# The first two batches' transposed activations and row of means: one by squares, one over memory, with ScalarE's work moved behind four projection steps

## The chip, the cores and the metric

The kernel runs on one core of a Trainium2 chip. Five engines work side by side and each executes its own instructions in order: TensorE (PE; its weight loads are listed as PEld), VectorE (DVE), ScalarE (ACT), GpSimd (POOL), and SyncE (SP), which here only issues DMAs. They are tied together by semaphores. The metric is the device time of one launch in microseconds, as the median of the runs shown.

## The reference

The input x has shape (16, 1024, 256), the adjacency `adj` is 1024x1024, everything is float32. Layer 0 is an attention whose queries come from a graph product; layer 1 is a two-layer graph network with batch norms. Both end in a residual and a layer norm. The change lies in the first microseconds of layer 0:

```python
fea = jnp.transpose(x, (0, 2, 1))
c_adj = jnp.mean(fea, axis=1)                       # mean of each node's 256 features
diff = c_adj[:, None, :] - c_adj[:, :, None]
A = jnp.abs(jnp.abs(jax.nn.sigmoid(diff) - 0.5) - 0.5) * 2.0
A_s = (A + jnp.transpose(A, (0, 2, 1))) * 0.5
Wg = adj[None, :, :] * A_s                          # 1024x1024 weights for each batch
g = jnp.einsum('bcn,bnm->bcm', fea, Wg)
g = jax.nn.relu(g * para.reshape(1, C, N))          # becomes the queries
kv = (x @ kv_w).reshape(B, N, 2, h, hd).transpose(2, 0, 3, 1, 4)
attn = jax.nn.softmax(jnp.einsum('bhnd,bhmd->bhnm', q, k) * scale, axis=-1)
```

The kernel computes the weights as abs(c_m - c_n), then tanh of half of it, then (tanh - 1) times the adjacency, with the sign put right later.

## The kernel before

`fast_path` does the work (`general_path` is a fallback that these inputs don't take). The 1024 nodes of a batch are 8 chunks of 128 partitions. For each batch `b` a function `prologue(b)` builds three lists of steps: `first` (the batch's x transposed, its means), `steps` (the projections: `values` and `keys`, four of each, and for batch 0 the graph product `graph_first`, eight chunks), and `side` (`weights_abs` and `weights_tanh` on ScalarE and `weights_adj` on VectorE for each of the eight chunks: the 128x1024 tiles `wg`). The main loop runs attention of batch b in bursts of two units (`scores` on PE, exp on ScalarE, `outputs` on PE, sums on VectorE) and works off the lists of batches b+1 and b+2 between the bursts. For batches 0 and 1 there is no attention to hide behind yet, so their lists are run in a block ahead of the loop, lines 1332 to 1348. There PE, ScalarE, VectorE and SP run exactly in the order of the program text, since the block stands under `manual_schedule`; GpSimd's order is left to a planner.

How the pieces concerned are made:

- **Means.** `begin` sums x over its features on VectorE (L796, `csum`), scales the sum to the column of means `ccol` (L798), and, for all batches but 0, to a negative copy in `ncol` (L801), which `column_to_row` transposes (L777) and writes to memory with four small DMAs (L780, `c`); a fifth DMA (L804) reads the row back into all 128 partitions as `crow`. For batch 0 the row is made by PE instead: `row_of_means` (L830) multiplies the transposed x by a constant matrix `ncmat`, eight matmuls into a PSUM tile.
- **Transposed x** (`xT`). For batches 0 and 1, `transpose_x` does four groups of four 128x128 PE transposes (L811), each group copied out of PSUM (L815) by VectorE, or by ScalarE for two groups of batch 1. From batch 2 on, `load_squares` (L764) loads x in 32x32 squares by four DMAs for each of two halves, and `transpose_squares` (L820) transposes a half in one VectorE instruction. Both halves pass through one buffer (tag `xS`, one deep), so the second load waits for the first transpose.
- **Buffers.** `wg` has eight buffers, so a tile of batch 1 can be begun only when PE is through with the same chunk of batch 0. Each of the PSUM tags `s`, `t`, `o` has two buffers; `values`, `keys` and `transpose_x` share tag `t`. VectorE copies batch 0's values out of PSUM (L1011), ScalarE the keys (L997).
- **Loads.** SP issues x of batch 0 in two halves, the projection weights `kvw_s`, two adjacency chunks, x of batch 1, the other six adjacency chunks and `para_s`, all ahead of the first step.

In the block before the loop, PE's order is: four transpose groups of batch 0, the row of means, four `values` and four `keys` in turn, four transpose groups of batch 1, the 64 matmuls of `graph_first` (L978), then batch 1's `values` and `keys`, then the first scores. ScalarE's and VectorE's weight steps are laid between these two at a time.

Of the kernel before, what the change touches and what calls it, by code (L numbers as in the profile page):

```python
# [10 lines left out]
F32 = mybir.dt.float32  # L11
# [7 lines left out]
P = 128  # L19
HALF = 512  # L20
# [495 lines left out]
def fast_path(  # L516
# [19 lines left out]
    nc = tc.nc  # L536
    B, N, C = x.shape
    H = 4
    D = C // H
    NCH = N // P  # L540
    CC = C // P
# [4 lines left out]
    const = ctx.enter_context(tc.tile_pool(name="const", bufs=1))  # L546
# [13 lines left out]
    def tile_s(name):  # L560
        return psum["s"].tile([P, N], F32, tag="s", name=name)

    def tile_t(name):
        return psum["t"].tile([P, HALF], F32, tag="t", name=name)
# [17 lines left out]
    make_identity(nc, ident)  # L582
    ones = const.tile([P, D], F32, name="ones")
    nc.gpsimd.memset(ones, 1.0)
    ncmat = const.tile([P, P], F32, name="ncmat")
    nc.gpsimd.memset(ncmat, -1.0 / C)
    mhalf = const.tile([P, NCH], F32, name="mhalf")
    nc.gpsimd.memset(mhalf, -0.5)

# [120 lines left out]
    def load_columns():  # L710
        for name, src, k in (
            ("b1", b1, HC), ("g1", g1, HC), ("be1", be1, HC),
            ("b2", b2, CC), ("g2", g2, CC), ("be2", be2, CC),
        ):
            cols[name] = const.tile([P, k], F32, name=f"col_{name}")
            nc.gpsimd.dma_start(cols[name], src.rearrange("(k p) -> p k", p=P))
# [9 lines left out]
    crp = graph.enter_context(tc.tile_pool(name="crp", bufs=1))  # L726
# [8 lines left out]
    with (  # L735
# [9 lines left out]
        adj_s = adjp.tile([P, NCH, N], F32, tag="adj", name="adj_s")  # L745
        para_s = pap.tile([P, CC, N], F32, tag="pa", name="para_s")
# [3 lines left out]
        def load_x(b):  # L750
            t = xp.tile([P, NCH, C], F32, tag="x", name=f"x_{b}")
            src = x[b].rearrange("(n p) c -> p n c", p=P)
            if b == 0:
                for n in range(0, NCH, 4):
                    nc.sync.dma_start(t[:, n : n + 4, :], src[:, n : n + 4, :])
            else:
                nc.sync.dma_start(t, src)
            st[b] = {"x": t}

        def load_squares(b, c):  # L760
            xs = st[b]["xS", c] = xsp.tile([P, N // SQ, SQ], F32, tag="xS", name=f"xS_{b}_{c}")
            src = x[b].rearrange("(j k) (c q i) -> c q k j i", k=SQ, q=NQ, i=SQ)
            for q in range(NQ):
                nc.sync.dma_start(xs[q * SQ : (q + 1) * SQ], src[c, q])  # L764
# [1 line left out]
        load_x(0)  # L766
        nc.sync.dma_start(kvw_s, kv_w.rearrange("(c p) k -> p c k", p=P))
        adj_src = adj.rearrange("(n p) m -> p n m", p=P)
        for n in range(0, NCH, 2):
            nc.sync.dma_start(adj_s[:, n : n + 2, :], adj_src[:, n : n + 2, :])  # L770
            if n == 0:
                load_x(1)
        nc.sync.dma_start(para_s, para.rearrange("o (c p) i j -> p (o c) (i j)", p=P))
        load_columns()

        def column_to_row(row_d):
            nc.vector.transpose(ncol[:, 1], ncol[:, 0])  # L777
            dst = row_d.rearrange("o (n q i) -> q (o n) i", q=NQ, i=SQ)
            for q in range(NQ):
                nc.sync.dma_start(dst[q], ncol[q * SQ : q * SQ + NCH, 1])  # L780

        def prologue(b):


            s = st[b]
            xt = s["x"]
            first, steps, side = [], [], []
# [4 lines left out]
            def begin():  # L792


                csum = small.tile([P, NCH], F32, tag="csum", name=f"csum_{b}")
                nc.vector.tensor_reduce(csum, xt, AX.X, ALU.add)  # L796
                s["ccol"] = small.tile([P, NCH], F32, tag="ccol", name=f"ccol_{b}")
                nc.vector.tensor_scalar(s["ccol"], csum, 1.0 / C, None, ALU.mult)  # L798
                if b == 0:
                    return  # L800
                nc.vector.tensor_scalar(ncol[:, 0, :NCH], csum, -1.0 / C, None, ALU.mult)  # L801
                column_to_row(c_d[b])
                s["crow"] = crp.tile([P, N], F32, tag="crow", name=f"crow_{b}")
                nc.sync.dma_start(s["crow"], c_d[b][0].partition_broadcast(P))  # L804

            def transpose_x(c, half):
                if c == 0 and half == 0:
                    s["xT"] = xTp.tile([P, CC, N], F32, tag="xT", name=f"xT_{b}")
                pt = tile_t(f"pxT_{b}_{c}_{half}")
                for j in range(4):  # L810
                    nc.tensor.transpose(  # L811
                        pt[:, j * P : (j + 1) * P], xt[:, 4 * half + j, c * P : (c + 1) * P], ident
                    )
                copy = nc.scalar.copy if half and b else nc.vector.tensor_copy
                copy(s["xT"][:, c, half * HALF : (half + 1) * HALF], pt)  # L815

            def transpose_squares(c):
                if c == 0:
# [1 line left out]
                nc.vector.transpose(  # L820
                    s["xT"][:, c, :], s["xS", c].rearrange("p j i -> p (j i)")
                )

            def row_of_means():

                s["crow"] = tile_s("crow_0")
                for half in range(2):
                    hs = slice(half * HALF, (half + 1) * HALF)
                    for c in range(CC):
                        nc.tensor.matmul(  # L830
                            s["crow"][:, hs], ncmat, s["xT"][:, c, hs],
                            start=(c == 0), stop=(c == CC - 1),
                        )


            def weights_abs(n):
                w = wgp.tile([P, N], F32, tag="wg", name=f"wg_{b}_{n}")
# [172 lines left out]
                copy = nc.scalar.copy if pair % 2 and b else nc.vector.tensor_copy  # L1010
                copy(s["v"][:, 2 * pair : 2 * pair + 2, :].rearrange("p n c -> p (n c)"), pt)  # L1011

            if b < 2:
                for i in range(2 * CC):
                    first.append((transpose_x, (i // 2, i % 2) if b else (i % 2, i // 2)))
            else:
                first += [(transpose_squares, (c,)) for c in range(CC)]
            if b == 0:
                first += [(begin, ()), (row_of_means, ())]
            else:  # L1020
                first.insert(0, (begin, ()))
            for i in range(4):
                step(values, i)
                step(keys, i // 2, i % 2)
# [9 lines left out]
            else:  # L1034
                a, t, j = weights_abs, weights_tanh, weights_adj
# [149 lines left out]
        def run(fs, k):  # L1185
            for f, a in fs[:k]:
                f(*a)
            del fs[:k]
# [135 lines left out]
        with tc.manual_schedule(  # L1324
# [5 lines left out]


            first, steps, side = prologue(0)
            run(first, 6)
            next_first, next_steps, next_side = prologue(1)
            for i in range(8):
                run(steps, 1)
                run(side, 2)
                if i == 4:
                    run(next_first, 1)
            run(next_first, 4)  # L1340
            for n in range(NCH):
                run(side, 2)
                run(steps, 1)
                if n:
                    run(next_side, 3)
            for _ in range(8):
# [42 lines left out]
            for j in range(len(bursts)):  # L1389
                b, u = j // PERB, j % PERB  # L1390
                for i in bursts[j]:
                    scores(i)
                if u == 0:
                    steps, side = next_steps, next_side
                    next_first, next_steps, next_side = [], [], []
# [4 lines left out]
                if u == 5 and b + 2 < B:  # L1400
                    load_x(b + 2)
                    next_first, next_steps, next_side = prologue(b + 2)
# [24 lines left out]
                elif u == 4:  # L1427
                    p = st[b + 1]["graph"]["p"]
# [7 lines left out]
                elif u == 8:  # L1436
                    p = st[b + 1]["graph"]["p"]
# [28 lines left out]
            j = len(bursts)  # L1466
# [51 lines left out]
    with (  # L1518
# [162 lines left out]
        for k in range(HC):  # L1681
            ps = [bank(f"ph_{k}_{half}") for half in range(2)]
            for half, hs in enumerate((H0, H1)):
                for c in range(CC):
                    nc.tensor.matmul(
                        ps[half], w1T[:, c, k * P : (k + 1) * P], t[:, c, hs],
                        start=(c == 0), stop=(c == CC - 1),
# [332 lines left out]
def kernel(tc: tile.TileContext, *args):  # L2020


    with tc.tile_pool(name="flag", bufs=1, space=DRAM) as flag:
        good_d = flag.tile([1, 1], I32, name="good_d")
        fast_path(tc, *args, good_d)
        good = tc.nc.values_load(good_d[0:1, 0:1], min_val=0, max_val=2 * P)
        with tc.If(good < 2 * P):
            general_path(tc, *args)
# [30 lines left out]
```

## Time and profile before

| | us |
|---|---|
| median of three runs (lowest, highest) | 2470.86 (2469.76, 2471.12) |
| the profiled execution's own time | 2469.28 |
| its span | 2467.5 |
| PE busy | 2425.2 (98% of the span) |
| VectorE busy | 1840.3 (75%) |
| ScalarE busy | 1231.6 (50%) |
| GpSimd busy | 479.9 (19%) |

The span is the profiled stretch from the first to the last instruction; the run's own time adds 1.8 us around it. A busy share is an average over very different stages, so what a change of the first stage is worth has to be read from that stage. An instruction group is named by line, engine, operation and output<-inputs; `SPq` marks the issuing of a DMA.

### The profile page before, as it was taken

The numbers are of one execution on the slowest core, as the hardware profiler recorded it, in microseconds if no ns is written. First come the engines' busy times: TensorE is split into PE (matmuls) and PEld (weight loads), VectorE is DVE, ScalarE is ACT, GpSimd is POOL, SyncE is SP. The second block draws the span as 40 slices with busy tenths as digits, with TensorE's granted clock in tenths as the row PEclk, the third lists the DMA queues.
The fourth block names the chain that finished last, engine by engine and source line by source line (L and its number), as shares of the span: only waits on it lengthen the run. The fifth ranks groups of instructions, "written<-read, shape, count | busy, mean of one in ns | idle before, by whom it ended". The sixth has DMA issues, their size and how long they took to land.

```text
span 2467.5 us, 32796 instructions
## 1 busy us (share of the span) xinstructions
PE 2425.2 (98%) x12462; PEld 1035.2 (42%) x12462; DVE 1840.3 (75%) x2528; ACT 1231.6 (50%) x1535; POOL 479.9 (19%) x487
## 2 busy tenths in 40 slices
PE   8999999999999999999999999999999999999997
PEld 4343443443434434434434343344444444434455
DVE  5678878878888888788788888856555555578568
ACT  6375665765765766757657667311010010144458
POOL 0021112211211211121112113522112212000026
PEclk9999999999999999999999999999999999999999
DMA  3123232332232231323322327222122122255559
GB/s 136 31 48 84 54 53 69 69 51 67 39 82 60 41 86 54 52 69 69 53 68 47 72 52 116 54 101 102 69 86 102 68 85 102 91 200 175 182 190 340
DMA packets 414647, 220.42 MB, mean 89 GB/s; under 512 B 353168, under 2 KB 386448, under 8 KB 406032
## 3 DMA queue, kind: packets, MB, share of 16 engines
q1 hardware_dynamic: 409120, 167.36, 27.6%
q0 software_dynamic: 4832, 50.34, 4.9%
q8 instruction: 100, 1.64, 0.3%
q14 instruction: 67, 0.55, 0.1%
q10 hardware_dynamic: 528, 0.52, 0.1%
HBM read 134.49 MB, written 83.69 MB: 88 GB/s over the span
## 4 chain that ended last, share of the span: by engine, by line
PE 83%; DVE 10%; ACT 3%; DMA 2%; issue 1%; SPq 0%; POOL 0%; DVEq 0%; POOLq 0%
PE ps L1066 17%; PE po L1087 17%; PE pgb L896 7%; PE b_agg L1564 4%; PE pga L896 4%; PE c_agg L1564 4%; PE pk L993 3%; PE po L1846 3%; PE pv L1006 2%; PE a_agg L1564 2%; PE b_h L1596 2%; PE b_o L1772 2%; PE pgc L896 2%; PE pgd L896 2%; PE c_h L1596 2%; PE c_o L1772 1%
## 5 line engine op out<-in xcount | busy, mean ns | idle before, releaser
L1071 ACT ACTIVATE p<-ps 128x1024 f32<-128x1024 f32 x512 | 497.4, 1021 | 182.2 <-PE ps L1066 123.2
L1097 DVE TENSOR_TENSOR acc<-acc,p 128x1024 f32<-128x1024 f32 x384 | 501.4, 1306 | 52.3 <-ACT p L1071 28.9
L1066 PE MATMUL ps<-qT,kT 64*64 64x512 f32 x4096 | 488.3, 592 | 0.3 <-ACT p L1071 0.3
L1087 PE MATMUL po<-p,v 64*64 64x512 f32 x4096 | 485.6, 589 | 0.0
L1161 POOL TENSOR_TENSOR o<-o,r_all 128x512 f32<-128x512 f32 x62 | 95.9, 1555 | 1104.8 <-DVE r_all L1155 989.9
L1087 PEld LDWEIGHTS po<-p,v 64*64 64x64 f32 x4096 | 159.4, 133 | 280.1 <-issue 273.2
L1066 PEld LDWEIGHTS ps<-qT,kT 64*64 64x64 f32 x4096 | 152.4, 133 | 285.9 <-issue 248.5
L847 DVE SCALAR_TENSOR_TENSOR wg<-wg,adj_s 128x1024 f32<-128x1024 f32 x128 | 149.7, 1217 | 24.6 <-ACT wg L843 24.6
L838 ACT ACTIVATE wg<-crow,ccol 128x1024 f32<-128x1024 f32 x128 | 146.7, 1146 | 6.1 <-PE pg L978 6.1
L843 ACT ACTIVATE wg<-wg 128x1024 f32<-128x1024 f32 x128 | 135.9, 1062 | 0.9
L993 PE MATMUL pk<-xT,kvw_s 128*128 128x512 f32 x256 | 121.9, 598 | 3.1 <-ACT drow L1140 3.1
L1006 PE MATMUL pv<-kvw_s,xT 128*128 128x256 f32 x512 | 123.9, 385 | 0.0
L1006 PEld LDWEIGHTS pv<-kvw_s,xT 128*128 128x128 f32 x512 | 95.0, 190 | 50.3 <-issue 13.6
L906 ACT ACTIVATE qT<-qT 128x512 f32<-128x512 f32 x60 | 37.1, 626 | 149.8 <-DVE qT L909 145.3
L896 PE MATMUL pgb<-wg,S 128*128 128x512 f32 x240 | 111.0, 605 | 0.0
L896 PE MATMUL pga<-wg,x 128*128 128x512 f32 x240 | 109.6, 599 | 0.7 <-ACT qT L919 0.7
L1564 PE MATMUL a_agg<-ahT,x1l 128*128 128x512 f32 x240 | 108.1, 593 | 0.7 <-ACT agg L1312 0.7
L1564 PE MATMUL b_agg<-aT,x1S 128*128 128x512 f32 x240 | 107.9, 592 | 0.0
L1162 POOL TENSOR_TENSOR x<-x,o 128x512 f32<-128x512 f32 x62 | 106.9, 1734 | 2.4
L656 ACT COPY p_agg<-a_agg 128x512 f32<-128x512 f32 x15 | 8.8, 586 | 183.3 <-PE a_agg L1564 179.5
L1675 ACT ACTIVATE hl<-hl,bn_sh,bn_sg 128x1024 f32<-128x1024 f32 x64 | 75.6, 1232 | 40.7 <-DMA hl<-h 38.1
L692 POOL TENSOR_TENSOR x1S<-x1l 128x512 f32<-128x512 f32 x15 | 19.4, 1293 | 352.9 <-PE c_agg L1564 350.1
(234 smaller groups left out, 3495.8 us busy)
## 6 DMA issues: line engine op xcount, KB each, us to landing
h<-hw POOLq DMA_DIRECT2D x16, 2048.0 KB, 6.6
hl<-h SPq DMA_DIRECT2D x32, 1024.0 KB
x<-x POOLq DMA_DIRECT2D x16, 1024.0 KB, 4.3
x1l<-x SPq DMA_DIRECT2D x16, 1024.0 KB
xf<-x SPq DMA_DIRECT2D x16, 1024.0 KB
o<-oS SPq DMA_DIRECT2D x62, 256.0 KB
o<-o SPq DMA_DIRECT2D x248, 64.0 KB
x<-in_x_dram SPq DMA_DIRECT2D x15, 1024.0 KB
```

The source lines that it names most:

```text
L838: nc.scalar.activation(w, s["crow"], AF.Abs, bias=s["ccol"][:, n : n + 1])
L843: nc.scalar.activation(w, w, AF.Tanh, scale=0.5)
L847: nc.vector.scalar_tensor_tensor(w, w, 1.0, adj_s[:, n, :], op0=ALU.subtract, op1=ALU.mult)
L896: nc.tensor.matmul(ps, left, right, start=(start and i == 0), stop=(i == NCH // 2 - 1), skip_group_check=True,)
L993: nc.tensor.matmul(ps, kvw_s[:, c, kc * P : (kc + 1) * P], s["xT"][:, c, hs], start=(c == 0), stop=(c == CC - 1),)
L1006: nc.tensor.matmul(pt[:, j * C : (j + 1) * C], s["xT"][:, c, n * P : (n + 1) * P], kvw_s[:, c, C : 2 * C], start=(c == 0), stop=(c == CC - 1),
L1066: nc.tensor.matmul(ps[kh * D : (kh + 1) * D, hd * HALF : (hd + 1) * HALF], kT[r, pr, ks], qT[r, pr, qh * HALF : (qh + 1) * HALF], start=Tr ...
L1071: nc.scalar.activation(p, ps, AF.Exp)
L1087: nc.tensor.matmul(g["po"][kh][hd * D : (hd + 1) * D, :], s["v"][r, m, h * D : (h + 1) * D], p[r, hd * HALF : (hd + 1) * HALF], start=(m = ...
L1097: nc.vector.tensor_add(g["acc"], g["acc"], p)
L1162: nc.gpsimd.tensor_tensor(xs, xs, o, ALU.add)
L1564: nc.tensor.matmul(ps, left, right, start=(start and i == 0), stop=(i == NCH // 2 - 1), skip_group_check=True,)
```

## The change

The row of means of batch 0 goes the way of the other batches' rows, by VectorE and memory, into a buffer taken from the pool of the attention's sums (`accp`, tag `acc`). `row_of_means` and its matrix go. Batch 1's transposed x is made from squares like that of later batches. ScalarE instead of VectorE copies batch 0's transposes. The six later adjacency chunks, batch 1's x and `para_s` are issued after batch 0's row. In the block, the weight steps of batch 0 begin at the fifth projection step (i = 4) and all that remain are issued ahead of the graph product; batch 1's `begin` stands at i = 6, its two square transposes at graph chunks 1 and 5.

```diff
-    ncmat = const.tile([P, P], F32, name="ncmat")
-    nc.gpsimd.memset(ncmat, -1.0 / C)
...
-        for n in range(0, NCH, 2):
-            nc.sync.dma_start(adj_s[:, n : n + 2, :], adj_src[:, n : n + 2, :])
-            if n == 0:
-                load_x(1)
-        nc.sync.dma_start(para_s, para.rearrange("o (c p) i j -> p (o c) (i j)", p=P))
+        nc.sync.dma_start(adj_s[:, :2, :], adj_src[:, :2, :])
         load_columns()
+
+        def load_rest():
+            for n in range(2, NCH, 2):
+                nc.sync.dma_start(adj_s[:, n : n + 2, :], adj_src[:, n : n + 2, :])
+                if n == 2:
+                    load_x(1)
+            nc.sync.dma_start(para_s, para.rearrange("o (c p) i j -> p (o c) (i j)", p=P))
...
-                if b == 0:
-                    return
                 nc.vector.tensor_scalar(ncol[:, 0, :NCH], csum, -1.0 / C, None, ALU.mult)
                 column_to_row(c_d[b])
-                s["crow"] = crp.tile([P, N], F32, tag="crow", name=f"crow_{b}")
+                pool, tag = (crp, "crow") if b else (accp, "acc")
+                s["crow"] = pool.tile([P, N], F32, tag=tag, name=f"crow_{b}")
                 nc.sync.dma_start(s["crow"], c_d[b][0].partition_broadcast(P))
...
-                copy = nc.scalar.copy if half and b else nc.vector.tensor_copy
-                copy(s["xT"][:, c, half * HALF : (half + 1) * HALF], pt)
+                nc.scalar.copy(s["xT"][:, c, half * HALF : (half + 1) * HALF], pt)
...
-            def row_of_means():
-
-                s["crow"] = tile_s("crow_0")
-                for half in range(2):
-                    hs = slice(half * HALF, (half + 1) * HALF)
-                    for c in range(CC):
-                        nc.tensor.matmul(
-                            s["crow"][:, hs], ncmat, s["xT"][:, c, hs],
-                            start=(c == 0), stop=(c == CC - 1),
-                        )
...
-            if b < 2:
+            if b == 0:
                 for i in range(2 * CC):
-                    first.append((transpose_x, (i // 2, i % 2) if b else (i % 2, i // 2)))
+                    first.append((transpose_x, (i % 2, i // 2)))
+                first.append((begin, ()))
             else:
+                first.append((begin, ()))
                 first += [(transpose_squares, (c,)) for c in range(CC)]
-            if b == 0:
-                first += [(begin, ()), (row_of_means, ())]
-            else:
-                first.insert(0, (begin, ()))
...
-            run(first, 6)
+            run(first, 5)
+            load_rest()
             next_first, next_steps, next_side = prologue(1)
             for i in range(8):
                 run(steps, 1)
-                run(side, 2)
-                if i == 4:
+                if i > 3:
+                    run(side, 2)
+                if i == 6:
                     run(next_first, 1)
-            run(next_first, 4)
+                    load_squares(1, 0)
+            run(side, 99)
             for n in range(NCH):
-                run(side, 2)
                 run(steps, 1)
+                if n in (1, 5):
+                    run(next_first, 1)
+                if n == 1:
+                    load_squares(1, 1)
                 if n:
                     run(next_side, 3)
```

## The prediction

> **What bounds the kernel now.** I read the page's busy times and chain shares first, to see which engine sets the length:
>
> ```profile
> PE 2425.2 (98%) x12462; PEld 1035.2 (42%) x12462; DVE 1840.3 (75%) x2528; ACT 1231.6 (50%) x1535; POOL 479.9 (19%) x487
> ...
> PE 83%; DVE 10%; ACT 3%; DMA 2%; issue 1%; SPq 0%; POOL 0%; DVEq 0%; POOLq 0%
> ```
>
> PE is busy for all but 42 us of 2467.5. So work taken from PE early moves everything later forward, unless PE then waits for what the work had covered. Next, the chain that ended last, asked for the first 160 us (columns: start, length, what):
>
> ```profile
> 5.04 3.45 PE pxT L811 x16
> 8.48 3.44 PE crow L830 x8
> 11.92 1.73 PE pv L1006 x8
> ...
> 27.48 0.67 PE pxT L811 x4
> ...
> 28.91 0.65 PE pxT L811 x4
> 29.57 27.47 PE pg L978 x64
> 57.04 1.73 PE pv L1006 x8
> ...
> 70.98 1.06 PE ps L1066 x8
> ```
>
> PE runs from 5.04 to the first scores at 70.98 nearly without a gap. Two stretches are what the change takes off PE: the row of means (3.44) and batch 1's transposes, from the end of the last keys at about 25.7 to the graph product at 29.57 (3.9, their waits included). Third, SyncE's timeline, for the DMAs (start, issue time), and ScalarE's, for what must now keep up:
>
> ```profile
> 24.01 1.35 SPq L780 DMA_DIRECT2D c<-ncol  x4
> 26.39 0.35 SPq L804 DMA_DIRECT2D crow<-c  x1
> ...
> 130.51 2.60 SPq L764 DMA_DIRECT2D xS<-in_x_dram  x4
> ```
>
> ```profile
> 11.83 1.28 ACT L838 ACT_TABLE_LOAD   x1 [11.83 <-DVE ccol L798]
> ...
> 31.24 1.06 ACT L843 ACTIVATE wg<-wg 128x1024 f32<-128x1024 f32 x1
> 32.20 1.13 ACT L838 ACTIVATE wg<-crow,ccol 128x1024 f32<-128x1024 f32 x1
> 33.37 1.06 ACT L843 ACTIVATE wg<-wg 128x1024 f32<-128x1024 f32 x1
> 34.33 1.13 ACT L838 ACTIVATE wg<-crow,ccol 128x1024 f32<-128x1024 f32 x1
> ```
>
> From the first write of the row to the issue of its read are 2.38 us; an abs and tanh pair takes 2.13 (32.20 to 34.33).
>
> [...]
>
> **The change, part by part.** I follow each engine through the new block. PE sets the end, so I look for where it would wait.
>
> *Transposes of batch 0.* x's second half is in before 6.9 us: PE's third group then waited for a copy and for no load. Copies by ScalarE take 0.59 (L815 in the timeline) for VectorE's 0.69, so the groups end at about 8.4 (was 8.48). Unknown: where the table load lands. In the record it stands behind a separate wait instruction and directly ahead of the abs. I take it to be hidden (in the idle 5 us at the start, or ahead of the first abs, where there is slack, below). The other end is that it sits behind the first transposes and delays all by 1.28.
>
> *Row of means, PE.* Eight matmuls leave: -3.44. The eight projection steps take 1.72 each, 13.8 together: 8.4 to 22.2.
>
> *Row of means, VectorE and SP.* VectorE has no copies ahead of `begin` now: sum 2.28 from about 6.4, scaling, copy and transpose bring it to 2.80 in all (21.18 to 23.98 for batch 1 before): 9.2. SP is free (its queue holds only x, weights and two adjacency chunks, 2.6 MB, which at the 250 to 380 GB/s of the one-microsecond windows end near 11). Writes issue at 9.2; +2.4: read issued at 11.6. Before, the read issued at 26.39 showed its traffic (139, 328 and 74 GB/s) in the windows from 27 to 30, so it lands at most 3.6 later: 15.2 here. The first values' copy (PE done at 10.1) finds VectorE free.
>
> *ScalarE behind four steps.* Its fifth step comes after the second keys' copy, 8.4 + 4 x 1.72 + 0.6 = 15.9. So the row (15.2) is there: abs and tanh 0 end at 18.1, or 19.4 with the table load. Then the third keys' copy (PE done 18.8), pair 1 to 21.7, abs 2, the fourth copy at 22.8, tanh 2 at 24.4, and pairs 3 to 7 at 2.13 each until 35.2. The copies matter since PE's fourth keys need the buffer of the third (20.5; copied by 19.5 to 20.1).
>
> *VectorE.* Behind the fourth values' copy (PE done 20.45, copied 21.15): adjacency step 0 (1.18) to 22.3. Then, in the same queue, batch 1's `begin`, 2.80, to 25.1, and only then step 1, to 26.3. Its sum waits for batch 1's x, now issued behind the row: 0.5 MB of row from 13.2, 1 MB of adjacency, 1 MB of x, at 0.33 to 0.4 MB per us, in by 20.6. It is wanted at 22.3: 1.7 to spare. Steps 2 to 7 follow ScalarE's pace and end at 36.4.
>
> *PE, graph product.* Chunk 0 starts at 22.3 (0.1 of waiting), ends 25.7; chunk 1 waits for step 1 until 26.3 (0.6). From there chunks need a tile every 3.43 us and get one every 2.13, chunk 7's being ready at 36.4 and wanted at 46.9. End: 26.3 + 7 x 3.43 = 50.3, against 57.04. **Gain 6.7**; 7.3 less the two waits.
>
> *Batch 1's squares.* Added: eight DMAs and two transposes of 1.22 (L820), no longer four ScalarE and VectorE copies. SP: the row of batch 1 [...] is read at 28.6, in at 32.2; ScalarE wants it at 35.2. The squares' issue follows, 2.6 us. Similar loads before took 5.5 (traffic from 130.5 until 136) to 8.2 us (144.8 until 153, mixed with another load). So half 0 is in at 35 to 37; its transpose stands behind adjacency step 7, done near 37.8. The one-deep buffer then lets half 1 go: in at 43.5 to 46, transposed by 47.2 at the latest, with two adjacency steps of batch 1 behind it, until 49.6. PE wants xT, and VectorE's queue empty for the queries, at 50.3. Hidden, with 0.7 to 3 us to spare. ScalarE's weights of batch 1, begun at 35.2, follow PE's release of buffers as before by 49.5.
>
> *The rest.* `ncmat`'s memset on GpSimd ran for 0.2 us beside the x load and is worth nothing. The row's buffer from tag `acc` is last read at 34 and first wanted by sums past 66. Loads of later batches keep their places relative to attention, and I find nothing tied to absolute time. So the 6.7 should pass through: span 2467.5 to 2460.8, own time 2469.28 to 2462.6. The median lies 1.6 above that execution: 2470.86 - 6.7 = 2464.2.
>
> **The rivals.**
>
> *Table load ahead of the first transpose copy* (12%). For: the compiler's load stands by the first ScalarE instruction that needs it, and a copy may count as one. Against: in the record it came after a split-off wait, and a copy has one wait only. Everything moves by 1.28; `begin`, not held up, keeps its time. 2465.5.
>
> *VectorE's queue is late for the queries or the values* (13%). For: slack after half 1 of the squares is 0.7 if its 128-byte rows run as slowly as at 144.8, and each further microsecond in either load counts, since they are in series. Against: DMA is otherwise empty then. If each is 2 us slower still, about 2.7 is lost: 2466.9.
>
> *The gain does not arrive* (6%). For: later stages have waits of their own (VectorE waited 2.15 us for adjacency squares at 1529), and ScalarE starts 3 us later than before, so it might become the bound. Against: tiles come faster than PE takes them, and the stage at 1529 follows PE's end of attention. 2470.9.
>
> *Slower* (5%). Batch 1's sum, in VectorE's queue ahead of adjacency step 1, takes over as the wait of the graph product: PE has chunk 0 and then nothing. Its x was landed early before and now stands behind the row's round trip over memory and SP's issue. For: before, SP took 5.93 us over three adjacency issues. Against: it was then throttled by earlier loads in flight. It decides when that x lands 6.7 later than 22.3, after 29; at 32, it costs 3: 2473.9.
>
> **How the numbers follow.** The forecast has 64%, gains of 6.0 to 7.3, 2463.5 to 2465. A measurement of this kernel can tell about 0.2%, 4.9 us, from no change; the forecast lies beyond it but by under 2 us. Faster: nearly all of the forecast (0.61), most of the table load (0.08), little of the third case (0.03): 0.72. Within: 0.22. Slower: 0.06. For the range I add 1 us of run-to-run difference below the full 7.3 (2462.5), and reach above to the late squares with the same on top (2468): all but the last two cases.
>
> **What would show it.** The graph product should begin at 22 to 23 and the first scores come at 64 to 65, after a stop of about half a microsecond behind chunk 0 put down to VectorE (L847). The projections should begin near 8.4; if at 9.7, the table load was in front. The first abs should begin at 15.9 to 17.3; if it waits for a DMA until past 19, the row's trip is longer than I have it. A sum at L796 that waits for x past 22.3, a second square transpose that ends after 48, or a wait of batch 1's values for VectorE are where the gain would be lost. Wrong altogether: scores 6.7 earlier but the end not.

## The result and the profile after

| | before | after |
|---|---|---|
| median of 8 runs (lowest, highest), us | 2470.70 (2469.76, 2471.75) | 2464.24 (2461.90, 2466.15) |
| ratio of the medians, with its 95% interval | | 0.9972 (0.9963 to 0.9981) |
| the profiled execution's own time; its span | 2469.28; 2467.5 | 2466.15; 2464.3 |
| first scores in the profiled execution | 70.98 | 64.97 |

The medians differ by 6.5 us (4.7 to 9.1 by the interval). The two profiled executions differ by only 3.1. That is not a contradiction, and it is taken up below: the first stage gained 6.0, and the last stages of one execution lie up to 3 us away from those of the next. A second set of runs of after on another chip (e7) lies 5.8 below before there.

The page of the kernel after, busy times and shares of the chain:

```profile
PE 2424.5 (98%) x12438; PEld 1032.6 (42%) x12438; DVE 1837.4 (75%) x2526; ACT 1232.4 (50%) x1537; POOL 479.8 (19%) x486
...
PE 83%; DVE 11%; ACT 2%; DMA 2%; issue 1%; SPq 1%; POOL 0%; POOLq 0%; DVEq 0%; ACTq 0%
```

PE executes 24 instructions fewer (8 for the row, 16 transposes) and its busy sum is 0.7 us smaller. The span is 3.2 shorter. So busy sums tell nearly nothing of what was won (matmuls at half rate, taken up below, count as longer work in them, 2.78 us for 16 score matmuls that take 1.95 at the full one), and the place has to be found in time. The chain that ended last, in the first 160 us of the kernel after (start, length, what):

```profile
5.08 3.73 PE pxT L811 x16
8.80 1.86 PE pv L993 x8
...
21.64 1.21 DVE wg L834
22.85 2.21 DVE csum L797
...
25.49 1.19 DVE wg L834
26.69 0.04 issue
26.73 24.30 PE pg L965 x56
51.03 1.73 PE pv L993 x8
...
64.97 1.06 PE ps L1051 x8
```

The row is gone from between the transposes and the first values, and batch 1's transposes from ahead of the graph product. The chain leaves PE in one place alone: VectorE makes adjacency step 0, sums batch 1's x, makes step 1, and only then do the 56 matmuls of chunks 1 to 7 run without a gap. PE is not idle all this while, it works on the last keys and on chunk 0. From the end of the last keys to that of the graph product it takes 28.32 us, and 27.46 in e4 (below), where it does not wait: so its two waits, ahead of chunk 0 and of chunk 1, are 0.9 together. SyncE's timeline of the kernel after, with the issue of batch 0's row (start, time of issue, what):

```profile
9.37 1.36 SPq L781 DMA_DIRECT2D c<-ncol  x4
12.36 0.35 SPq L804 DMA_DIRECT2D crow<-c  x1
```

Its ScalarE timeline (start, busy, what; in brackets the idle time before it and what ended it):

```profile
0.73 1.28 ACT L814 ACT_TABLE_LOAD   x1 [0.73 <-PEq L2037]
6.20 0.59 ACT L814 COPY xT<-pxT 128x512 f32<-128x512 f32 x1 [4.19 <-PE pxT L811]
...
16.87 1.15 ACT L825 ACTIVATE wg<-crow,ccol 128x1024 f32<-128x1024 f32 x1 [0.42 <-DMA crow<-c]
18.05 1.06 ACT L830 ACTIVATE wg<-wg 128x1024 f32<-128x1024 f32 x1
```

The table load stands in the idle time ahead of the first copy. The first abs waits 0.42 us for the row, and its tanh is done at 19.1, while VectorE takes adjacency step 0 up at 21.64: for that step the row could have come some 2.5 us later. Whether it could for ScalarE's next work too was not tested: the third keys' copy stands behind this tanh, at 19.30. VectorE's timeline of the kernel after, where batch 1's squares are transposed:

```profile
37.91 1.25 DVE L819 STREAM_TRANSPOSE xT<-xS 128x1024 f32<-128x1024 f32 x1 [1.51 <-DMA xS<-in_x_dram]
...
44.79 1.25 DVE L819 STREAM_TRANSPOSE xT<-xS 128x1024 f32<-128x1024 f32 x1 [2.01 <-DMA xS<-in_x_dram]
45.96 2.31 DVE L834 SCALAR_TENSOR_TENSOR wg<-wg,adj_s 128x1024 f32<-128x1024 f32 x2
49.35 2.48 DVE L952 SCALAR_TENSOR_TENSOR qT<-pg,para_s 128x512 f32<-128x512 f32 x4 [1.08 <-PE pg L965]
```

Both transposes wait for their load, and what stands behind them in the lists waits with them: the tanh for the first of the two adjacency steps was done at 43.65, and the step runs at 45.96, behind the transpose. But the queries (L952) then wait for PE, by 1.08 us. The squares are hidden, narrowly.

The 6.0 us pass through the attention of the first 15 batches whole: the first denominator of the last batch comes at 1508.88 before and at 1502.88 after.

### The profile page after: what moved, and what is told of

Its sections match the earlier page's. It is cut to its first block, busy times and chain, and to the rows that moved or that the text cites. A ratio compares the mean times of both kernels' runs of the same rounds, so it can differ in the third digit from the quotient of the medians.

```text
span 2464.3 us, 32766 instructions
## 1 busy us (share of the span) xinstructions
PE 2424.5 (98%) x12438; PEld 1032.6 (42%) x12438; DVE 1837.4 (75%) x2526; ACT 1232.4 (50%) x1537; POOL 479.8 (19%) x486
## 4 chain that ended last, share of the span: by engine, by line
PE 83%; DVE 11%; ACT 2%; DMA 2%; issue 1%; SPq 1%; POOL 0%; POOLq 0%; DVEq 0%; ACTq 0%
PE ps L1051 17%; PE po L1072 17%; PE pgb L883 7%; PE b_agg L1555 4%; PE pga L883 4%; PE c_agg L1555 4%; PE pk L980 4%; PE po L1837 3%; PE pv L993 3%; PE a_agg L1555 2%; PE b_h L1587 2%; PE pgd L883 2%; PE pgc L883 2%; PE b_o L1763 2%; PE c_h L1587 2%
```

## The experiments

Theory: the gain is work taken off PE ahead of the first scores, it arrives whole at the end, and what is left of it to win is VectorE's order (the sum in front of adjacency step 1). Rivals: one part of the change does all of it; the squares have no slack; the row's trip over memory decides, through the order of SyncE's queue. "After" and "before" name the two kernels; every kernel is compared with runs of before on its own chip. ScalarE's later start and its copies of batch 0's transposes were not tried alone.

| run | what it is | median (runs) | before there | ratio (95%) | first scores |
|---|---|---|---|---|---|
| e1 | after, eight row matmuls back on PE | 2466.76 (21) | 2471.61 | 0.9983 (0.9977 to 0.9990) | 69.20 |
| e2 | after, batch 1 transposed by PE | 2466.72 (16) | 2471.61 | 0.9981 (0.9973 to 0.9988) | 68.28 |
| e3 | before, squares for batch 1 | 2467.76 (21) | 2471.61 | 0.9983 (0.9976 to 0.9990) | 67.47 |
| e4 | after, batch 1's sum later | 2464.03 (10) | 2471.61 | 0.9974 (0.9964 to 0.9983) | 64.00 |
| e5 | after, second square load twice | 2465.87 (12) | 2470.89 | 0.9981 (0.9973 to 0.9990) | 67.14 |
| e6 | after, bulk loads ahead of the row | 2475.78 (21) | 2470.89 | 1.0020 (1.0014 to 1.0027) | 76.97 |
| e7 | after, again | 2465.10 (10) | 2470.89 | 0.9976 (0.9966 to 0.9985) | 66.16 |
| e8 | e4, again | 2463.62 (7) | 2470.89 | 0.9970 (0.9959 to 0.9981) | 65.15 |
| e9 | e4, fillers at two waits | 2464.43 (8) | 2471.43 | 0.9972 (0.9961 to 0.9982) | 65.03 |
| e10 | e4, again | 2463.73 (6) | 2471.43 | 0.9968 (0.9956 to 0.9981) | 64.01 |
| e11 | e4, the last filler alone | 2462.79 (6) | 2471.25 | 0.9967 (0.9955 to 0.9979) | 63.98 |
| e12 | e4, again | 2462.73 (6) | 2471.25 | 0.9967 (0.9955 to 0.9979) | 64.97 |

First scores of one kernel differ between executions: 64.97 and 66.16 for after, 64.00, 65.15, 64.01 and 64.97 for e4. By the pace of its matmuls PE begins each of these executions at about half rate, and the trace has records of the clock granted to it, as a share of the full one: full rate came at 8.74 us in after and at 11.15 in e7. Half of that difference of 2.4 is the difference of 1.2 in the first scores. In before's profile it came at 7.95, the earliest of all 14; there one transpose of batch 0 followed another every 0.21 us ahead of that record and every 0.11 behind it.

### The two parts, each alone

e1 puts eight matmuls of the removed row's shape back in its place; nothing reads their result, they are extra work. (The row itself still goes over memory.)

```diff
+            def row_unused():
+                ps = tile_s("row_unused")
...
+                        nc.tensor.matmul(
+                            ps[:, hs], ident, s["xT"][:, c, hs],
...
-                first.append((begin, ()))
+                first += [(begin, ()), (row_unused, ())]
...
-            run(first, 5)
+            run(first, 6)
```

> The kernel after, with eight matmuls of the old row of means put back on PE in their old place (their result is unused; nothing else moves). If PE's time is what the change saved (my theory): projections begin 3.4 us later than in the kernel after (8.8 to 12.2), VectorE's adjacency steps follow them, first scores near 68.4 instead of 65.0, and the whole about 3.4 above the kernel after, 3 below the kernel before. If the block is set by ScalarE's and VectorE's weights or by the loads (rival), the matmuls hide in waits: under 1 us, first scores before 66.

The chain of e1:

```profile
8.71 4.45 PE row_unused L821 x8
13.15 1.73 PE pv L1003 x8
...
30.96 24.30 PE pg L975 x56
...
69.20 1.06 PE ps L1061 x8
```

The scores come 4.2 later than in after, not 3.4: the eight matmuls took 4.45, since PE's clock reached its full rate only in the middle of them in this execution, at 10.62. Everything behind them kept its distance (values to scores: 56.05 here, 56.17 after). The median rose less than that, by 2.5 against the 8 runs of after and by 1.7 against e7, both on other chips. Its runs had a higher clock: 15 of 21 show a mean granted clock of 0.998, of before's 57 only one. Compared at 0.996, where before has 50 runs, e1's runs are 2.7 below it (2468.89 to 2471.59), near what is expected with the row paid and the rest kept; but they are only two. Why adding matmuls here lifted the mean clock stays open.

e2 leaves the row's change and takes back the squares; e3 is the squares alone, in the kernel before.

```diff
-                first += [(transpose_squares, (c,)) for c in range(CC)]
+                if b == 1:
+                    first += [(transpose_x, (i // 2, i % 2)) for i in range(2 * CC)]
+                else:
+                    first += [(transpose_squares, (c,)) for c in range(CC)]
```

> The kernel after, with batch 1's x transposed by PE again between the last keys and the graph product (copies by ScalarE), no squares for batch 1; so this is the row part alone. Theory: four groups end about 3.7 after the last keys (22.5 to 26.3) but cover the wait for adjacency steps 0 and 1, so the graph product loses 3.0 and not 3.9; first scores near 68.0, 3.0 above the kernel after. Rival, that squares cost as much on VectorE and DMA as they save on PE: no difference.

```diff
-            if b < 2:
+            if b == 0:
...
-            run(next_first, 4)
...
+                    load_squares(1, 0)
...
+                if n in (1, 5):
+                    run(next_first, 1)
+                if n == 1:
+                    load_squares(1, 1)
```

> The kernel before, with batch 1's x from squares and nothing else changed (row of means on PE, ScalarE's steps where they were); the squares part alone. Theory: the graph product begins right behind the last keys, at 25.7 instead of 29.6, and finds its tiles ready; first scores near 67.2, 3.8 below the kernel before. With the run before this makes 3.4 + 3.8 = 7.2, less what the two parts share, 6.5. Rival, that the two parts only work together (weights late or squares late): under 2 us.

The chain of e2, in which ScalarE copies batch 1's transposes behind the weight steps laid before them:

```profile
24.24 0.96 ACT wg L830
25.19 0.48 ACT xT L814
...
25.72 1.14 PE pxT L811 x8
26.87 27.47 PE pg L965 x64
...
68.28 1.06 PE ps L1054 x8
```

The chain of e3:

```profile
24.35 1.72 PE pk L993 x4
26.07 27.47 PE pg L978 x64
...
67.47 1.06 PE ps L1066 x8
```

The row alone wins 2.7 at the first scores (70.98 to 68.28), the squares alone 3.5, both at once 6.0.

These figures hold a piece of chance, since PE came to its full rate at 7.95 in before but at 10.05 in e2, 8.66 in e3 and 8.74 in after. It can be taken out by an estimate: the transposes of all three took 0.3 longer than before's 3.45, e2's first `values` group took 2.44 where later ones take 1.73, and that of after 1.86. Then the row alone is worth 3.7, the squares alone 3.8, and both at once 6.4. So neither part is the whole, and together they win 1.1 less than their sum of 7.5: about the wait for VectorE, which stands in the chain of neither e2 nor e3, and which e4 takes away for 1.0. So it was expected with e3: 7.2, less what the parts share, 6.5.

The medians show the overlap too, if not to a microsecond: 4.9 and 3.9 below before, at equal clock (0.996) 4.3 and 3.8, against 5.8 to 6.5 for both at once on other chips. e3 also shows what the squares do by themselves: the graph product's 64 matmuls follow the fourth keys directly, with no gap at all.

### The sum that stands in front of adjacency step 1

e4 lays the steps so that VectorE makes adjacency steps 0 and 1 before batch 1's `begin`.

```diff
                 if i > 3:
-                    run(side, 2)
+                    run(side, (2, 3, 3, 0)[i - 4])
```

> The kernel after, with adjacency steps 0 and 1 of batch 0 each one projection step earlier in VectorE's and ScalarE's lists, so that batch 1's sum no longer stands between them. Theory: the wait of the graph product behind chunk 0 goes, first scores near 64.1 instead of 65.0, about 0.9 less in all. Rival, that batch 1's row and with it the squares come later by the same and are waited for: no gain, or a loss.

The chain of e4:

```profile
20.88 1.72 PE pk L980 x4
22.60 27.47 PE pg L965 x64
...
64.00 1.06 PE ps L1051 x8
```

VectorE is gone from the chain; PE runs from 5.00 to the scores with nothing in between. The profile gains 1.0 over after. The squares, by contrast, have less slack here: the queries wait for PE by 0.30 us alone. Beside after on one chip (e7, e8) the medians stand 1.5 apart, where 0.9 was expected, and with e10 and e12 all four medians of this kernel are 7.3 to 8.5 below before on their chips, where after's two are 6.5 and 5.8 below. The best version found is this one; its intervals overlap those of after, so that it is the better one rests on the chain and on four medians, not on one ratio.

> The kernel after itself, in more runs beside the kernel before and the other kernels of this call, since the runs of one kernel spread over 4 to 6 us. Theory: the first scores come 6.0 earlier and nothing later depends on it, so the medians differ by 6.0, give or take 1. Rival, that a later stage takes part of it back: under 4.

> The kernel with adjacency steps 0 and 1 earlier (batch 1's sum behind them), once more beside the kernel after on the same chip: theory, 0.9 below it, as the first scores were at 64.0 for 65.0; rival, that the stages of the last batch, which wait for DMAs and VectorE, swallow a microsecond: equal.

### How much slack the squares have

e5 issues the second half's load twice, the same bytes into the same buffer (the second time is extra).

```diff
+        def load_again(b, c):
+            xs = st[b]["xS", c]
+            src = x[b].rearrange("(j k) (c q i) -> c q k j i", k=SQ, q=NQ, i=SQ)
+            for q in range(NQ):
+                nc.sync.dma_start(xs[q * SQ : (q + 1) * SQ], src[c, q])
...
                     load_squares(1, 1)
+                    load_again(1, 1)
```

> The kernel after, with the second half of batch 1's squares loaded twice in a row into the same buffer, which makes its transpose 4.5 to 7 us later (44.8 in the kernel after; here 49 to 52) and nothing else. By the queues' order (theory) the transpose holds up two adjacency steps and the queries behind it on VectorE, these hold up the copy of the first values, and PE waits for that copy: of the delay about 2 us are slack, the rest arrives: first scores 2.5 to 5 later than 65.0. If squares have slack to spare or VectorE's order is of no weight (rival): no more than 0.5.

VectorE's timeline of e5:

```profile
48.12 1.25 DVE L825 STREAM_TRANSPOSE xT<-xS 128x1024 f32<-128x1024 f32 x1 [5.30 <-DMA xS<-in_x_dram]
...
51.53 2.48 DVE L958 SCALAR_TENSOR_TENSOR qT<-pg,para_s 128x512 f32<-128x512 f32 x4
```

The second load costs 3.3 (44.79 to 48.12), and the queries come 2.2 later than in after (49.35 to 51.53), now without a wait for PE. So 1.1 of the delay was swallowed, which is the 1.08 us that the queries waited for PE in after. PE then waits as expected for VectorE's copy of the first values, 1.26 us by its timeline. All three sizes had been put too high: the load at 4.5 to 7, the slack at 2, the scores at 2.5 to 5. The scores move by the same 2.2, and the median by 0.8 against e7 and by 2.1 where both have a clock of 0.996 (2467.16 to 2465.10). So squares slower by more than 1.1 us are paid for.

### The order of SyncE's queue

e6 issues the other adjacency chunks, batch 1's x and `para_s` ahead of the row, where before had them.

```diff
+            load_rest()
             run(first, 5)
-            load_rest()
```

> The kernel after, with the six later adjacency chunks, batch 1's x and the last parameter issued ahead of batch 0's row, as in the kernel before, and nothing else. If small writes queue behind loads issued earlier (theory): the row is written when these loads are done, near 25, read back by 29, ScalarE's first abs starts near 28.7 instead of 16.9, the third keys' copy behind it in its queue holds PE, the graph product starts 9 later and first scores come near 74, past the kernel before's 71.0. If a small DMA passes loads in flight (rival): first scores within 1 us of 65.0.

SyncE's timeline of e6:

```profile
12.32 2.49 SPq L781 DMA_DIRECT2D c<-ncol  x4
25.86 0.35 SPq L804 DMA_DIRECT2D crow<-c  x1
```

The chain of e6:

```profile
14.52 11.19 DMA c<-ncol
...
25.86 3.38 DMA crow<-c
...
29.32 1.16 ACT wg L825
...
32.87 30.16 PE pg L965 x64
...
76.97 1.06 PE ps L1051 x8
```

The row's writes are issued 3 us later than in after because SyncE is held up in the loads' issue (7.75 us over the last two pairs of adjacency chunks, which took 1.44 in after), and their read follows 13.5 us behind them (12.32 to 25.86) where it was 3.0 in after (9.37 to 12.36). ScalarE starts its weights at 29.32 and the graph product begins ten microseconds later than in after.

It also runs slower, 30.16 for 27.47 in e4, since PE's clock had dropped in the wait: the clock records have it at half rate from 27.55 to 37.79. That is most of the 3 us by which the scores come later than expected (74). One link of the expectation failed: the third keys' copy did come late, at 31.46, but the fourth keys had run at 22.57, so it did not hold PE, which waited 8.32 us for adjacency step 0 instead.

The kernel is 4.9 slower than before, 10.7 slower than after. So the move of the loads, an inconspicuous part of the diff, carries more than the whole gain: without it the change loses. The small writes, issued behind the loads, landed only when these were done, and that has a price: those 13.5 us against 3.0. The loads' traffic, 416 GB/s between 22 and 24 us, ends before 25, and the last write is in at 25.71.

### Why executions of one kernel differ by more than what is looked for

In the profiled execution of after the last stages gave back 2.8 of the 6.0. One of the places shows when PE's timelines are laid beside those of e7, the same kernel. After:

```profile
1534.39 1.86 PE L1119 MATMUL den<-acc,ones 128*32 128x512 f32 x4 [1.84 <-DVE acc L1082]
1536.19 2.78 PE L1051 MATMUL ps<-qT,kT 64*64 64x512 f32 x16
```

e7:

```profile
1535.48 1.05 PE L1119 MATMUL den<-acc,ones 128*32 128x512 f32 x4 [1.76 <-DVE acc L1082]
1536.47 1.95 PE L1051 MATMUL ps<-qT,kT 64*64 64x512 f32 x16
```

The same instructions after nearly the same wait, and in one execution they take 1.86 and 2.78, in the other 1.05 and 1.95. The table by windows of after tells why (stretch, us; busy time and count of PE, PEld, DVE, ACT and POOL; PE's granted clock; share of DMA, GB/s):

```profile
1531.09:1534.50 3.41, 1.57 (x14) 0.25 (x8) 3.24 (x7) 3.18 (x5) 1.21 (x1) 1.00 0.64 267
1534.50:1537.91 3.41, 3.41 (x12) 0.59 (x15) 3.24 (x10) 0.59 (x1) 1.64 (x1) 0.50 0.20 77
```

For 3.41 us PE ran at half rate, behind a wait of 1.84 us. From the last batch's first denominators to the first `pw` matmuls after them it was 41.17 us here (1502.88 to 1544.05) and 39.45 in e7 (1504.04 to 1543.49): this stretch costs some 1.7. By the clock records after had three of them (from 1534.50, 2179.62 and 2374.18), before's profile none until 2455.3. After's lead over before falls nearly by these alone: it is 6.0 us at the denominators, 5.3 at the `pw` matmuls, 4.2 behind the second stretch and 2.8 behind the third. So the profile of before, with a mean clock of 0.998 that one of its 57 runs on another chip reached, was a lucky one beside that of after, with 0.996.

By the clock records each of the three stretches of after lasted 3.413 us, and their starts lie whole multiples of that apart: 189 of them between the first two (645.12 us), 57 between the last two (194.56). So the execution can be cut into windows of 3.413 us, counted from the clock records, and what went ahead of a stretch can be read from them. The first line above is such a window, and here is the one with the same wait in e7:

```profile
1533.50:1536.91 3.41, 1.65 (x10) 0.35 (x12) 3.24 (x6) 2.18 (x4) 0.85 (x1) 1.00 0.48 199
```

PE was busy for 1.57 us of the window in after, and half rate followed; for 1.65 in e7, and it did not. In all 14 profiles, up to 2445 us, half rate followed each of the 21 windows at full rate in which PE was busy for up to 42% of the time, three of the eight between 43 and 48%, and none of the others. No idle gap as long as a window was needed: the wait was 1.84 us ahead of the stretch shown here. What sets the clock was not shown beyond these counts. Since the windows start at another time in each execution (1531.09 in after, 1533.50 in e7), one wait can fall into one window or be split over two.

Could the stretches be avoided? e9 puts matmuls of no use, whose results nothing reads, into two of e4's waits: six in the last denominators' and 24 transposes of the identity in the last stage's. e11 has the second filler alone.

```diff
+                if i == 2 and k == B * PAIRS - 2:
+                    for _ in range(6):
+                        nc.tensor.matmul(
+                            den[64:96, :], ones[:, :32], G[b, pr, 0]["acc"][:, :HALF],
+                            start=True, stop=True,
+                        )
...
+                            if b == 0 and pair == 0 and j == 0 and c == 1:
+                                for _ in range(24):
+                                    nc.tensor.transpose(pt[:, P : 2 * P], ident, ident)
```

> The kernel with adjacency steps 0 and 1 earlier, and with work of no use laid on PE in two places where it waits in every kernel and where half-rate stretches were seen to follow: six small matmuls in the wait of the last batch's first denominators (1.8 to 2.7 us near 1535), 24 transposes of the identity in the wait of the last stage (3.0 us near 2372). If PE's idle time brings on a half-rate stretch of 3.4 us (theory), the stretches near 1535 and 2374 do not occur, the runs' mean granted clock rises by about 0.001, and the time falls by 1 to 2 us against the same kernel without fillers. If the stretches have another cause (rival), they stay, and the time is the same or up to 1 us longer.

> The same kernel without the fillers, beside it on the same chip: 7.3 below the kernel before, mean granted clock mostly 0.996 to 0.997, half-rate stretches near 2374 and in some runs near 1535.

> The kernel with adjacency steps 0 and 1 earlier and the 24 identity transposes in the wait of the last stage alone; the six matmuls near 1535, which took 3.9 us for a wait of 1.8 to 2.9, are left out again. Theory (idle PE time brings on the half-rate stretch): no stretch near 2374, the last stage's first group 1.5 us shorter, as with both fillers, and now nothing lost elsewhere: 1.0 to 1.5 below the same kernel without fillers, about 8.5 below the kernel before. Rival (stretches and time are unrelated, or the stretch is put off to later): the same time.

> The same kernel without filler, beside it: 7.3 below the kernel before.

PE's timeline of e10 in the last stage, with a stretch behind the wait:

```profile
2374.37 1.76 PE L1918 MATMUL pf<-ident,o 128*128 128x128 f32 x7 [2.98 <-ACT o L1894]
2375.91 2.70 PE L1935 MATMUL held<-ident,o 128*128 128x128 f32 x16
```

The same lines of e12, the same kernel:

```profile
2371.21 0.98 PE L1918 MATMUL pf<-ident,o 128*128 128x128 f32 x7 [2.98 <-ACT o L1894]
2372.03 1.95 PE L1935 MATMUL held<-ident,o 128*128 128x128 f32 x16
```

Two equal waits of 2.98 us, and 1.5 us between them in what follows. The windows that hold most of the wait, in e10 and then in e12:

```profile
2370.65:2374.06 3.41, 0.73 (x3) 0.14 (x1) 2.01 (x6) 2.73 (x4) 0.55 (x1) 1.00 1.00 423
```

```profile
2369.25:2372.66 3.41, 1.45 (x13) 1.46 (x14) 1.31 (x5) 2.73 (x4) 0.47 (x1) 1.00 0.86 363
```

In e10 nearly the whole wait lies in one window. In e12 a boundary falls into the wait, and the window still held 1.45 us of work, which is 43%. Of the four profiles of this kernel without filler, e8 and e10 have this last stretch, e4 and e12 have not.

In the two with fillers no half-rate stretch followed a filled wait (e11 had one elsewhere, from 2175.42), and their runs have mean clocks of 0.997 and 0.998, while all six of e10 have 0.996. Yet there is no gain in the medians. e9 is 0.7 above e10: between the denominators and the `pw` matmuls it took 41.8 us where e12, with no stretch there, took 39.3, so the first filler costs 2.6, more than a stretch does. e11 is level with e12, three of whose six runs have the higher clock without any filler. That the last filler is worth the 1.0 to 1.5 expected of it has not been shown; with six runs each it is not excluded either.

## Why the prediction was right

The forecast was 2464.2 and the median 2464.24. That is closer than the working deserves, and luck: at the first scores the change won 6.0 where 6.7 were forecast, the medians' difference has an interval of 4.7 to 9.1, and on another chip it was 5.8. The mechanism held: work came off PE, and what was left on the path was VectorE's order. Step by step:

- **Transposes of batch 0.** The projections began at 8.80, not 8.4. 0.3 of it is PE's clock at the start (16 transposes in 3.73 rather than 3.45, full rate at 8.74 rather than 7.95); the table load was at 0.73, so the hidden end of that unknown was the true one, and the rival built on the other end is out.
- **Row of means over memory.** Writes issued at 9.37 (9.2), read at 12.36 (11.6), first abs at 16.87 (15.9). The trip was mis-sized twice: issue to issue took 3.0 where I took over 2.4 from batch 1 of before, and from the read's issue to the first abs it took 4.5 where I had at most 3.6 (in e6, with no load issued behind it, 3.4). It stayed off the path all the same. The 2.4 count from the first of four writes; the last was issued by 25.4, 1.0 ahead of the read. And the fourth keys' need of the third's buffer did not show in e6.
- **VectorE ahead of the graph product.** Step 0 ended at 22.85 (22.3), the sum did not wait for x, chunk 1 began at 26.73 (26.3). The sum in front of step 1 was indeed what was left on the path, and e4 takes it away for 1.0; the two waits measured 0.9 where I had booked 0.7. The slower rival needed x to land past 29 and x was there at 22.85. The slow issue that spoke for it did not come back: the three pairs of adjacency chunks that took SyncE 5.93 us in before, behind earlier loads, took 0.43 and 1.44 in after.
- **Graph product.** 56 matmuls took 24.30 against 7 x 3.43 = 24.0; it ended at 51.03 (50.3). These 0.3 and the 0.4 by which chunk 1 began late are the whole of the 0.7 that the scores fall short.
- **Batch 1's squares.** By SyncE's timeline its row was read at 30.40, not 28.6, 4.8 us after its writes, which stood behind the loads. The transposes ended at 39.16 and 46.04, within "near 37.8" plus 1.4 and "at the latest 47.2". I gave 0.7 to 3 us of slack; it is 1.1, by the wait in after and by e5. This rival was nearest to deciding. Its sum does not follow from its figures: two loads 2 us slower each, less 0.7 of slack, lose 3.3 and not 2.7.
- **The rest passes through.** It does to the last batch's denominators, at 1502.88 against 1508.88. What I did not have is that a single execution's last stages move by 3 us with the clock, so the own time of the profiled execution, forecast at 2462.6, came to 2466.15 while the median came out right.

## What to carry to other kernels

Where one engine is busy nearly throughout, follow each engine's instructions in program order through the changed block and ask where the bound engine will wait: two such waits were foreseen here, 0.7 us together where 0.9 were measured, and the larger (a long reduction placed in front of the step that the bound engine needs) was then removed by one line. A small transfer that something waits for belongs ahead of bulk loads in its queue; here that order alone was worth 10.7 us, more than the whole change (2.7 of it by PE's clock, which fell in the long wait). And differences of one or two microseconds are to be read from the place in the trace where they arise, not from the end of one profiled execution.

## What was not expected of the hardware

PE fell to half its clock for 3.41 us, in e6 for three times that (10.24), behind each of 21 windows of 3.41 us in which it had been busy for up to 42% of the time and behind three of eight with 43 to 48%. A wait of 1.84 us was enough in one profile of after, and one of 1.76 in the other was not; 2.98 us were enough in e10 and not in e12, the same kernel; and 2.69 were not in before. At the places compared above a stretch cost 0.7 to 1.7 us. Before's 57 runs on one chip spread from 2468.93 to 2474.84, and their medians by mean clock fall in order: 2474.0 at 0.995 (2 runs), 2471.6 at 0.996 (50), 2470.0 at 0.997 (4), though the one run at 0.998 took 2472.3. At the start of a launch PE reached its full rate at times from 7.95 to 11.15 us in the 14 profiles, though its first matmul came between 4.92 and 5.19 in all of them, and the first scores moved with it (64.97 for 8.74 in after, 66.16 for 11.15 in e7). ScalarE's table load ran at 0.73 us, ahead of every wait, when its first instruction was a copy; in before, where that was an abs, it ran at 11.83, behind the wait.
